# Factor layout, swapped reciprocals and an earlier normalisation in a two-layer graph kernel

## The chip, the cores and the metric

The kernel runs on one core of a Trainium2 chip. A core has five engines that run side by side, each with its own queue of instructions: TensorE for matrix products (PE in the profile, with PEld for loading its weights), VectorE (DVE), ScalarE (ACT), GpSimd (POOL) and SyncE (SP, which here only issues DMAs). ACT issues DMAs as well. The metric is the device time of one execution in microseconds (us), a median over runs.

## What is computed

`x` is 64 graphs of 256 nodes with 512 channels; all graphs share one adjacency matrix. Both layers add a graph layer's output to their input and normalise each row:

```python
# layer 0: a sum over the neighbours, as two products of x
Wi, Wj = (W[:, :Din], W[:, Din:])
mi = jnp.einsum('bkd,od->bko', x, Wi)
mj = jnp.einsum('bkd,od->bko', x, Wj)
out = deg[None, :, None] * (mi + b) + jnp.einsum('ij,bjo->bio', a, mj)
...
# layer 1: attention of 8 heads of 64 channels, masked by the graph
scores = jnp.einsum('bhqd,bhkd->bhqk', q, k) * scale
scores = jnp.where(mask, -jnp.inf, scores)
attn = jax.nn.softmax(scores, axis=-1)
out = jnp.einsum('bhqk,bhkd->bhqd', attn, v)
return out @ Wo.T + bo
...
x = _layernorm(x + layer0(x)); x = _layernorm(x + layer1(x))
```

q, k and v are products of the normalised first layer (called h) with 512 x 512 weights, plus biases. All is in 32 bit floats.

## The kernel before

Two graphs ("batches", index i) are a group g; there are 32 groups. A batch has two tiles of 128 nodes (t = 1 is made before t = 0). The main loop (L1109) runs over the groups. Each turn does the attention of group g (scores, exponentials, values and the division by the softmax sums, eight steps w of two heads each) and, between these, layer 0 of the two batches b1 and b2 of the next group. At its end stand the output projection of group g (`o_steps`), then the v, q and k projections of the next group. Nearly every instruction is recorded with `in_order`, which keeps each engine's instructions in the order of the program text; so that text is each engine's queue, and a wait holds up all that stands behind it on its engine.

**Products in three passes.** The four projections of layer 1 run in fp32r, a faster format of fewer bits than f32. So both sides are split into a head, a low and a diff part. The three products head x head, low x lift and diff x diff go to two PSUM banks: X takes the first and the second, Y the third, and the result is UP times X, plus Y. On the side of the weights the parts (head, lift, diff) are called a factor: 128 rows of 3 x 512 numbers, 16 of them for wv, wq, wk and wo. They are made once, stored to DRAM by `end_makes` into `kept`, and read again in each turn by `bring`, which issues one load of 768 KB on ACT's queue. The ring `stream` has six buffers; `bring` waits until the matmuls have let go of the oldest. For v all four factors are in use at once, and for the output projection too. The parts of the activations are `hP` (tiles hA, hL, hD) for h, and `aoP` for the attention's output `aoT`, whose parts live in buffers that others have left: its head is called qT in the profile, its diff kT, its low part v.

**Banks.** `pair(kind)` takes an X and a Y bank: "S" takes one double bank of the two that the scores use too, "M" takes two of the three single banks, "A" one single bank and the bank of the values. In the profile a matmul into an "S" pair shows as pxy, into the others as px and py. A pair is free again when its two adds have been done (`add_x`, `add_y` in `o_steps`, `v_evict` for v).

**The output projection.** `o_steps` gives three steps: `o[0]` and `o[1]` make tiles 0 and 1 of the group's first batch, 12 matmuls each, with kinds "S" and "M"; `o[2]` makes both tiles of the second batch, 24 matmuls, kinds "A" and "S". Its adds go to DVE, and into `xh`, the residual. `v_pair` follows, kinds "SM" for the first batch (t = 1 takes "M" and comes first) and "AS" for the second (t = 1 takes "S" and comes first).

**How h comes to hP.** A tile is normalised in two parts: `stat` (DVE statistics, then rstd on POOL, L482) and `give` (a shift and a scaling on ACT, L487 and L488). `send_h` (L687) writes it to DRAM, `fetch_h` (L692) reads it back as hB in another order, `turn_h` transposes it on DVE (L506) into hF, and `split_head`, `split_diff`, `split_low` (L665, L668, L671) make its parts. In `o[2]`, between the matmuls, `turn` is called for tile 1 of b2, and its transpose stands on DVE ahead of the adds of the second batch.

**The division.** `values` leaves 128 rows per two steps w: four blocks of 32 channels, for which `channels(q)` gives the order. `divide_two` copies them to `aoT` on ACT; `divide` has PE sum the exponentials of the four heads (tile den, rows of 32 partitions for each), takes the reciprocal on DVE (L974, tile rden) and spreads it by four DMAs (L979) so that each of the four blocks and both of the two steps has its head's reciprocal (tile spread). `multiply` (L925, POOL) then multiplies. Two divisions are made for each batch. For the last of a turn ACT issues half of the DMAs.

The order at the end of a turn, with the lines that the prediction goes through:

```python
        values(g, 7)
        aoP[g][1], = three(("v",))
        split_low(*ao_parts(g, 0, every), nc.gpsimd)
        stat2(1)
        total_up = divide_two(g, 7)
        stat2(0)
        split_low(*ao_parts(g, 1, upper), nc.gpsimd)
        give2(1)
        give2(0)
```

`every`, `upper` and `lower` are all four channel chunks c, the first two, and the last two.

Of the kernel before, what the change touches and what calls it, by code (L numbers as in the profile page):

```python
# [16 lines left out]
P = 128  # L17
# [207 lines left out]
def unshifted_path(ctx, tc, flag, x, adj, wiT, wjT, b0, wqT, bq, wkT, bk, wvT, bv, woT, bo, out):  # L225
# [56 lines left out]
    def in_order(ins):  # L282

        tc.keep_in_program_order(ins)
# [90 lines left out]
    def channels(q):  # L375

        half, j = divmod(q, 2)
        return slice(j * DH + half * R, j * DH + (half + 1) * R)

    def load_wo(t, c0):  # L380
        w = woT.rearrange("(c p) o -> p c o", p=P)
        for q in range(P // R):
            in_order(nc.sync.dma_start(out=t[q * R:(q + 1) * R], in_=w[channels(q), c0:c0 + t.shape[1], :]))

    def small_loads():
        with nc.allow_non_contiguous_dma(reason="512 numbers, once"):
            for q in range(P // R):
                in_order(nc.sync.dma_start(out=bv_t[q * R:(q + 1) * R],
                                           in_=bv.rearrange("r (c p) -> p (r c)", p=P)[channels(q)]))
        in_order(nc.sync.dma_start(out=bo_bc, in_=bo.to_broadcast([P, D])))  # L390
        return load_bias(bq, "bq"), load_bias(bk, "bk")

# [1 line left out]
    bo_bc = const.tile([P, D], F32, name="bo_bc")  # L394

    weights = {"wq": wqT, "wk": wkT, "wv": wvT, "wo": woT}
    kept = {name: dram.tile([NC, P, 3, D], F32, tag=name, name=name) for name in weights}

    raws = {}

# [30 lines left out]
    def bring(several=1, left=1):  # L431
        for _ in range(several):
            if queue:
                name, j, first = queue.pop(0)
                f = stream.tile([P, 3, D], F32R, tag="factor", name="factor")
                coming.append(f)
                if first:
                    begin_make(f, name, j)
                    end_makes(left)
                else:  # L440
                    end_makes()
                    in_order(nc.scalar.dma_start(out=f.bitcast(F32), in_=kept[name][j]))

    def cut(f):
        return [f[:, i, :].rearrange("p (c o) -> p c o", c=NC) for i in range(3)]
# [10 lines left out]
    def end_makes(left=0):  # L456
        while len(started) > left:
            f, low, name, j = started.pop(0)
            head, lift, diff = cut(f)
            in_order(nc.scalar.activation(lift, low, AF.Identity, scale=LIFT))  # L460
            in_order(nc.vector.scalar_tensor_tensor(diff, low, LIFT, head.bitcast(F32), ALU.mult, ALU.subtract))
            in_order(nc.sync.dma_start(out=kept[name][j], in_=f.bitcast(F32)))

    def fold_value_bias():

# [337 lines left out]
                    v_evict(g, i, t, banks[t])  # L803
        return run

    def o_steps(g, kinds, turn):
        parts = aoP[g]

        def add_x(i, t, banks):
            r = xh[NB * g + i][:, t, :]  # L810
            in_order(nc.vector.scalar_tensor_tensor(r, banks[0], UP, r, ALU.mult, ALU.add))

        def add_y(i, t, banks):
            r = xh[NB * g + i][:, t, :]
            in_order(nc.vector.tensor_add(r, banks[1], r))

        def one(t):
            def run():
                banks = pair(kinds[t])
                for which in ((0, 1), (2,)):  # L820
                    for c in range(NC):
                        rows_of_product(banks, parts, t, coming[c], c, which)
                add_x(0, t, banks)
                add_y(0, t, banks)
            return run

        def two():
            banks = [pair(kinds[NT + t]) for t in range(NT)]
            for c in range(NC):
                for which in ((0, 1), (2,)):  # L830
                    for t in range(NT):
                        rows_of_product(banks[t], parts, NT + t, coming[0], c, which)
                coming.pop(0)
                if c:
                    bring()
                if c == 1:
                    bring()
                    h1 = turn(1)
                    split_head(*h1)
                    split_low(*h1, nc.gpsimd)  # L840
            add_x(1, 0, banks[0])
            split_diff(*h1)
            add_y(1, 0, banks[0])
            add_x(1, 1, banks[1])
            add_y(1, 1, banks[1])
            split_three(*turn(0), nc.gpsimd)

        return [one(0), one(1), two]

    def finish_steps(g):  # L850

# [56 lines left out]
    def values(g, w):  # L908
        i, pr = divmod(w, NC)
        if w == 0:  # L910
            aoT[g] = p1.tile([P, NC, NB * N], F32, tag="aoT", name="aoT")
        pp = w % 2
        if pp == 0:
            pavs[g] = value_bank("pav").rearrange("p (r q) -> p r q", r=2)
        pe, _ = made[g, w]
        for kc in range(NT):
            for q in range(P // R):
                d0 = 2 * pr * DH + channels(q).start
                matmul(pavs[g][q * R:(q + 1) * R, pp, :], vv[g][:, i, kc, d0:d0 + R], pe[:, q % 2, kc, :],
                       start=(kc == 0), stop=(kc == NT - 1), tile_position=(0, q * R))  # L920

    def multiply():
# [4 lines left out]
    def divide_two(g, w):  # L927

        dst = target(g, w)
        last = w == NB * NC - 1 and g < NG - 1  # L930
        in_order(nc.scalar.copy(dst, pavs[g]))
        i, pr = divmod(w, NC)
        return divide(dst, [made.pop((g, w - 1))[1], made.pop((g, w))[1]],
                      rtot[:, NB * g + i, pr // 2:pr // 2 + 1], last)

    def total(rden, total_out):
        unused = p1.tile([P, N], F32, tag="unused", name="unused")
# [2 lines left out]
    def divide_at_once(g, w):  # L940


        den = score_bank("den").rearrange("p (r q) -> p r q", r=2)
        for pp in range(2):
            _, pk = made.pop((g, w - 1 + pp))
            for q in range(P // R):
                matmul(den[q * R:(q + 1) * R, pp, :], ones[:, :R], pk[:, q % 2, :], start=True, stop=True,
                       tile_position=(0, q * R))
        inverses = p1.tile([P, 2, N], F32, tag="spread", name="rden")
        for pp in range(2):  # L950
            in_order(nc.vector.reciprocal(inverses[:, pp, :], den[:, pp, :]))
            in_order(nc.vector.tensor_mul(target(g, w)[:, pp, :], pavs[g][:, pp, :], inverses[:, pp, :]))
        return inverses
# [7 lines left out]
        cols = slice(i * N, (i + 1) * N)  # L961
        return cut_parts(aoP[g], cs, cols), aoT[g][:, cs, cols]

    def divide(dst, pks, total_out, last):


        den = bank("den")[:, :N]
        for pp in range(2):
            for j in range(2):
                q = 2 * pp + j  # L970
                matmul(den[q * R:(q + 1) * R, :], ones[:, :R], pks[pp][:, j, :], start=True, stop=True,
                       tile_position=(0, q * R))
        rden = p1.tile([P, N], F32, tag="rden", name="rden")
        in_order(nc.vector.reciprocal(rden, den))  # L974
        spread = p1.tile([P, 2, N], F32, tag="spread", name="spread")
        for half in range(2):
            for pp in range(2):
                issuer = nc.scalar if last and pp else nc.sync
                in_order(issuer.dma_start(out=spread[half * DH:(half + 1) * DH, pp, :],  # L979
                                          in_=rden[pp * DH:(pp + 1) * DH, :]))  # L980
        products.append((dst, spread))
        if last:
            return lambda: total(rden, total_out)
        total(rden, total_out)
# [18 lines left out]

    def projection_steps(g, kinds="", paired=True):
        if paired:
            v = [v_pair(g, 0, "MS"[::-1], False), v_pair(g, 1, "AS", True)]
        else:
            v = [v_step(g, i, t, kinds[NT * i + t], (i, t) == (NB - 1, 0)) for i in range(NB) for t in range(NT)]
        q, k = ([qk_step(g, store, tag, bias, m, kinds[m]) for m in range(NC)]
# [99 lines left out]
    for g in range(NG - 1):  # L1109
# [71 lines left out]
        values(g, 6)  # L1181
        values(g, 7)
        aoP[g][1], = three(("v",))
        split_low(*ao_parts(g, 0, every), nc.gpsimd)
        stat2(1)
        total_up = divide_two(g, 7)
        stat2(0)
        split_low(*ao_parts(g, 1, upper), nc.gpsimd)
        give2(1)
        give2(0)  # L1190
        total_up()
        send_h(b2, 1)
        send_h(b2, 0)
        fetch_h(b2, 1)
        fetch_h(b2, 0)
        split_diff(*ao_parts(g, 1, upper))
        if g + 2 < NG:
            next_p[0][2]()
        h10 = turn_h(b1, 0)
        multiply()  # L1200
        split_head(*ao_parts(g, 1, lower))
        split_head(*h10)
        p, q = next_p, next_q
        v, q_, k = projection_steps(g + 1)
        end = finish_steps(g)
        o = o_steps(g, "SMAS", lambda t: turn_h(b2, t))
        o[0]()
        split_diff(*ao_parts(g, 1, lower))
        split_low(*ao_parts(g, 1, lower), nc.vector)
        split_diff(*h10)  # L1210
        split_low(*h10, nc.vector)
        o[1]()
        run([o[2], v[0]])
        sum_x(b3)
        v[1]()
        turn_x(b3 + 1)
# [107 lines left out]
```

## Time and profile before

| what | value |
|---|---|
| time, median of 3 runs | 2985.07 us (2984.91 to 2987.25) |
| the profiled execution, its own time | 2979.46 us |
| its span, from the first to the last instruction | 2977.2 us |
| granted TensorE clock, mean | 0.998 |
| PE busy / PEld busy | 2934.5 us (99%) / 1917.7 us (64%) |
| DVE / ACT / POOL busy | 2310.1 (78%) / 1194.6 (40%) / 1273.0 us (43%) |
| queue q10 (ACT's DMAs) | 75,808 packets, 391.02 MB, 34.5% of 16 engines |
| queue q1 (SP's DMAs) | 229,584 packets, 215.69 MB, 25.1% |
| hB<-h_cols, issue to landing | 2.5 us least, 3.1 median, 8.0 most |
| one SP issue of spread<-rden | 0.59 us median, 446 of them (62 more on ACT) |

A row of a timeline is: start in us, duration in us, engine, line, operation, output<-inputs by the program's names, shapes, and in brackets how long the engine had been idle and who released it. A row of the waits is: engine, the tile that its instruction writes, its line, the releaser, then us in total, times, longest. "PE MATMUL pxy<-factor,qT" is a matmul of the output projection (with kT: diff; with v: low), "pxy<-factor,hA" (hD, hL) one of the v projection, "pxy<-hA,factor" one of q or k. The line L290 is the helper that records every matmul, so matmuls are told apart by their tiles. A matmul's record is longer than the distance to the next one's start, since they are pipelined; distances between starts say what PE spends.

### The profile page before, as it was taken

The page shows a single profiled execution, that of the slowest core. Times are in us where ns is not written, and L with a number is a line of the kernel's source. Part 1 is how long each engine was busy: PE and PEld are TensorE (multiplying, and loading weights), DVE is VectorE, ACT ScalarE, POOL GpSimd, SP SyncE. Part 2 cuts the span into 40 slices and gives each one's busy share as a digit, 9 for nine tenths or more (in the row PEclk, how much of TensorE's full clock was granted, in tenths as well). Part 3 has the DMA queues.
Part 4 walks back from the last instruction along what each step waited for, and adds up shares of the span by engine and source line. Part 5 has one row for each costly group of instructions (what it writes and reads, how often), then busy time and mean ns, then how long its engine had stood idle before and what let it go on. Part 6 is the DMA issues. An engine that isn't in the chain of part 4 may idle for free. (4 is left out here: it accounts for less than half of the span.)

```text
span 2977.2 us, 42690 instructions
## 1 busy us (share of the span) xinstructions
PE 2934.5 (99%) x15694; PEld 1917.7 (64%) x15694; DVE 2310.1 (78%) x3497; ACT 1194.6 (40%) x2243; POOL 1273.0 (43%) x950
## 2 busy tenths in 40 slices
PE   9999999999999999999999999999999999999998
PEld 5566666666666666666666666666666666666655
DVE  5977787777887778877778777788777787777875
ACT  3433434434434334343343343443433434334333
POOL 3534444344444344443444444444434444344443
PEclk9999999999999999999999999999999999999999
DMA  6566655667555665556665566755566555666553
GB/s 230 172 231 237 217 162 185 222 234 240 178 179 197 235 239 202 167 188 229 236 237 164 177 211 231 245 184 170 197 237 238 201 160 191 232 237 236 166 167 125
DMA packets 305604, 609.48 MB, mean 205 GB/s; under 512 B 27632, under 2 KB 189424, under 8 KB 305136
## 3 DMA queue, kind: packets, MB, share of 16 engines
q10 hardware_dynamic: 75808, 391.02, 34.5%
q1 hardware_dynamic: 229584, 215.69, 25.1%
q8 instruction: 126, 2.06, 0.3%
q14 instruction: 86, 0.70, 0.1%
HBM read 494.67 MB, written 78.64 MB: 193 GB/s over the span
## 5 line engine op out<-in xcount | busy, mean ns | idle before, releaser
L897 POOL TENSOR_TENSOR pk<-pe 128x512 f32<-128x512 f32 x256 | 330.7, 1303 | 534.6 <-ACT pe L887 534.6
L290 PE MATMUL po<-w,xS 128*128 128x512 f32 x992 | 466.1, 602 | 1.5 <-DVE mj L570 1.5
L290 PE MATMUL po<-w,xT 128*128 128x512 f32 x808 | 387.4, 604 | 0.8 <-ACT u L549 0.8
L482 POOL TENSOR_TENSOR rstd<-ve,mhalf 128x1 f32<-128x1 f32 x256 | 155.3, 607 | 493.1 <-DVE below L480 491.9
L887 ACT ACTIVATE pe<-pe 128x1024 f32<-128x1024 f32 x256 | 270.6, 1057 | 148.2 <-DVE pe L883 148.2
L671 POOL TENSOR_TENSOR hL<-hF,hA 128x512 fp32r<-128x512 f32 x93 | 151.2, 1626 | 387.5 <-ACT hA L665 387.5
L290 PEld LDWEIGHTS po<-w,xS 128*128 128x128 f32 x992 | 177.8, 189 | 214.6 <-issue 162.2
L883 DVE TENSOR_TENSOR pe<-ps,maskT 128x1024 f32<-128x1024 f32 x256 | 300.9, 1196 | 3.6 <-PE ps L290 3.6
L759 DVE TENSOR_TENSOR kT<-py,kT 128x512 f32<-128x512 f32 x128 | 88.5, 691 | 259.7 <-ACT kT L758 259.7
L290 PEld LDWEIGHTS po<-w,xT 128*128 128x128 f32 x808 | 145.6, 189 | 180.5 <-issue 179.0
L367 POOL TENSOR_TENSOR xh<-xh,degb 128x1024 f32<-128x1024 f32 x64 | 152.4, 2382 | 254.9 <-DMA xh<-in_x_dram 134.8
L290 PE MATMUL ps<-qT,kT 64*128 64x256 f32 x2048 | 256.5, 389 | 0.0
L290 PE MATMUL pav<-pe,v_sb 128*32 128x256 f32 x4096 | 248.7, 382 | 3.5 <-DVE kT L759 1.5
L290 PEld LDWEIGHTS ps<-qT,kT 64*128 64x128 f32 x2048 | 187.0, 186 | 69.0 <-PE pav L290 38.7
L487 ACT ACTIVATE shift<-below,rstd 128x1 f32<-128x1 f32 x256 | 74.5, 291 | 386.3 <-POOL rstd L482 231.2
L974 DVE RECIPROCAL rden<-den 128x256 f32<-128x256 f32 x127 | 221.9, 1747 | 6.3 <-PE den L290 3.8
L290 PEld LDWEIGHTS pav<-pe,v_sb 128*32 128x32 f32 x4096 | 118.3, 109 | 155.4 <-issue 49.2
L488 ACT ACTIVATE xh<-xh,shift,rstd 128x512 f32<-128x512 f32 x256 | 208.9, 816 | 8.5
L925 POOL TENSOR_TENSOR aoT<-aoT,spread 128x512 f32<-128x512 f32 x127 | 205.7, 1620 | 6.9 <-DMA spread<-rden 5.9
L665 ACT ACTIVATE hA<-hF 128x512 fp32r<-128x512 f32 x124 | 77.8, 628 | 287.1 <-DVE hF L506 231.5
L290 PE MATMUL px<-hA,factor 128*128 128x512 f32 x640 | 184.3, 410 | 0.0
L290 PE MATMUL py<-hD,factor 128*128 128x512 f32 x640 | 176.3, 397 | 2.2 <-ACT kT L758 2.2
(142 smaller groups left out, 6060.1 us busy)
## 6 DMA issues: line engine op xcount, KB each, us to landing
factor<-wv ACTq DMA_DIRECT2D x124, 768.0 KB, 6.3
factor<-wq ACTq DMA_DIRECT2D x124, 768.0 KB, 6.6
factor<-wk ACTq DMA_DIRECT2D x124, 768.0 KB, 6.4
factor<-wo ACTq DMA_DIRECT2D x120, 768.0 KB, 7.2
xB<-in_x_dram SPq DMA_DIRECT2D x256, 128.0 KB, 3.7
xh<-in_x_dram SPq DMA_DIRECT2D x64, 512.0 KB, 8.9
h_cols<-xh SPq DMA_DIRECT2D x124, 256.0 KB, 2.3
hB<-h_cols SPq DMA_DIRECT2D x124, 256.0 KB, 3.1
```

Of the source, the lines that this page charges most:

```text
L290: in_order(nc.tensor.matmul(*args, **kw))
L367: in_order(nc.gpsimd.tensor_tensor(xh[b], xh[b], degb, ALU.add))
L482: order(nc.gpsimd.tensor_tensor(rstd, ve, mhalf, ALU.pow))
L488: order(nc.scalar.activation(t, t, AF.Identity, bias=shift, scale=rstd))
L665: in_order(nc.scalar.activation(parts[0], src, AF.Identity, scale=DOWN))
L671: in_order(engine.tensor_tensor(parts[1], src, parts[0].bitcast(F32), ALU.subtract))
L759: in_order(nc.vector.tensor_add(dst, Y, dst))
L883: in_order(nc.vector.tensor_add(pe.rearrange("p j t q -> p j (t q)"), ps.rearrange("p j t q -> p j (t q)"), maskT.rearrange("p t q -> p (t ...
L887: in_order(nc.scalar.activation(flat, flat, AF.Exp, scale=QSCALE, accum_out=etot[:, NB * g + i, pr:pr + 1]))
L897: in_order(nc.gpsimd.tensor_tensor(pk, pe[:, :, 0, :], pe[:, :, 1, :], ALU.add))
L925: in_order(nc.gpsimd.tensor_tensor(d, d, spread, ALU.mult))
L974: in_order(nc.vector.reciprocal(rden, den))
```

## The change

- The factors in DRAM change from `[NC, P, 3, D]` to `[NC, 3, P, D]`: the three parts of a partition's row no longer lie beside each other, so that each piece in DRAM is 512 numbers, 2 KB, instead of 6 KB. The tile in SBUF is as before.
- The reciprocals are swapped rather than spread: `values` puts the two lower blocks (q = 2, 3) of the two steps in each other's place (`pp ^ (q // 2)`), so that the sums' reciprocals already fit one of the two slots where they stand. They are written to `spread[:, 0]`, and two DMAs, one for each half of the partitions, fill slot 1 with the other half's. The tile rden is gone. The same swap of channels goes into the loading of wo and of the value bias (`chunk_sets`), and into `divide_at_once`. One division near the end uses the buffer "lo".
- At the end of a turn `give2(1)` moves ahead of `divide_two(g, 7)`, and `send_h(b2, 1)` right behind it; `fetch_h(b2, 0)` moves behind the turning of h10 and the multiply.
- The low part of `aoP` for the first batch is made in two pieces, `upper` and `lower`, with `give2(1)` between them.
- `o_steps` gives `own`, `adds` and `others`. `own` makes both tiles of the first batch into "S" pairs, the low products of tile 0 put between and behind the first products of tile 1; `adds(0)` now stands ahead of `turn_h(b1, 0)` on DVE. `others` takes "A" and "M". The v pairs are "SS" and "AM" (with "AM", t = 1 takes "M" and comes first).

```diff
+    def chunk_sets(q):
+        return ((0, 1), (1, 0)) if q > 1 else ((0, 0),)
...
-    kept = {name: dram.tile([NC, P, 3, D], F32, tag=name, name=name) for name in weights}
+    kept = {name: dram.tile([NC, 3, P, D], F32, tag=name, name=name) for name in weights}
...
-                    in_order(nc.scalar.dma_start(out=f.bitcast(F32), in_=kept[name][j]))
+                    in_order(nc.scalar.dma_start(out=f.bitcast(F32), in_=kept[name][j].rearrange("k p d -> p k d")))
...
-            in_order(nc.sync.dma_start(out=kept[name][j], in_=f.bitcast(F32)))
+            in_order(nc.sync.dma_start(out=kept[name][j].rearrange("k p d -> p k d"), in_=f.bitcast(F32)))
...
+        def own():
+            for n, cs in ((0, (0, 1)), (1, (2, 3))):
+                banks[n] = pair("S")
+                times(n, range(NC), (0, 1))
+                times(0, cs, (2,))
+            times(1, range(NC), (2,))
+
+        def adds(n):
+            add_x(n)
+            add_y(n)
+
+        def others():
+            banks.update({2: pair("A"), 3: pair("M")})
...
-                matmul(pavs[g][q * R:(q + 1) * R, pp, :], vv[g][:, i, kc, d0:d0 + R], pe[:, q % 2, kc, :],
+                matmul(pavs[g][q * R:(q + 1) * R, pp ^ (q // 2), :], vv[g][:, i, kc, d0:d0 + R], pe[:, q % 2, kc, :],
...
-        rden = p1.tile([P, N], F32, tag="rden", name="rden")
+        spread = p1.tile([P, 2, N], F32, tag="lo" if other else "spread", name="spread")
+        rden = spread[:, 0, :]
         in_order(nc.vector.reciprocal(rden, den))
-        spread = p1.tile([P, 2, N], F32, tag="spread", name="spread")
         for half in range(2):
-            for pp in range(2):
-                issuer = nc.scalar if last and pp else nc.sync
-                in_order(issuer.dma_start(out=spread[half * DH:(half + 1) * DH, pp, :],
-                                          in_=rden[pp * DH:(pp + 1) * DH, :]))
+            issuer = nc.scalar if last and half else nc.sync
+            in_order(issuer.dma_start(out=spread[half * DH:(half + 1) * DH, 1, :],
+                                      in_=spread[(1 - half) * DH:(2 - half) * DH, 0, :]))
...
-            v = [v_pair(g, 0, "MS"[::-1], False), v_pair(g, 1, "AS", True)]
+            v = [v_pair(g, 0, "SS", False), v_pair(g, 1, "AM", True)]
...
-        split_low(*ao_parts(g, 0, every), nc.gpsimd)
+        split_low(*ao_parts(g, 0, upper), nc.gpsimd)
         stat2(1)
+        give2(1)
+        split_low(*ao_parts(g, 0, lower), nc.gpsimd)
         total_up = divide_two(g, 7)
+        send_h(b2, 1)
         stat2(0)
         split_low(*ao_parts(g, 1, upper), nc.gpsimd)
-        give2(1)
         give2(0)
         total_up()
-        send_h(b2, 1)
         send_h(b2, 0)
         fetch_h(b2, 1)
-        fetch_h(b2, 0)
         split_diff(*ao_parts(g, 1, upper))
         if g + 2 < NG:
             next_p[0][2]()
+        own, adds, others = o_steps(g, lambda t: turn_h(b2, t))
+        own()
+        adds(0)
         h10 = turn_h(b1, 0)
         multiply()
         split_head(*ao_parts(g, 1, lower))
         split_head(*h10)
+        fetch_h(b2, 0)
...
-        o[0]()
         split_diff(*ao_parts(g, 1, lower))
         split_low(*ao_parts(g, 1, lower), nc.vector)
         split_diff(*h10)
         split_low(*h10, nc.vector)
-        o[1]()
-        run([o[2], v[0]])
+        adds(1)
+        others()
+        v[0]()
```

## The prediction

> **What bounds the kernel now.** Parts 1 and 2 of the page come first: PE is busy 99% of the span, and the granted clock is 9 tenths or more in every slice. Part 4 (the chain that ended last) names only the last layer norm, so it doesn't help. The Trainium skill ("Perfetto Trace Analysis", Identifying the Most-Contended Engine) says that matmul busy time is a poor measure of how near PE is to its peak, since matmuls are pipelined. The trace agrees in a way that matters here: weight loading (PEld) is at 64%, and matmuls of 0.39 us start every 0.227 us. Busy time would leave under 43 us to gain (2977.2 - 2934.5). So I read starts in the timeline instead. Each turn of the main loop has the same 142 stretches of matmuls; at their undisturbed intervals (0.227 us for 512 columns of fp32r, 0.429 for a record of f32, and the usual 1.93, 1.75 and 0.55 us for a group of scores, values and sums) they need 88.07 us. The 29 periods measured from the trace take 90.7 us at least and 91.6 on average, in all 102 us over the ideal. About 77 us of it repeats every period (2.6 each), 25 us does not.
>
> Where is it? In PE's waits, these three kinds lead:
>
> ```profile
> PE pxy L290 <- DVE xh L815: 7.9, 4, 3.1
> PE pxy L290 <- POOL v L671: 6.5, 31, 0.9
> PE px L290 <- DMA factor<-wv: 4.1, 8, 1.0
> ```
>
> All three lie in the output projection and the v projection behind it. I call the first matmul of `o_steps` the boundary, and count us from it; the one at 1238.53 is undisturbed. PE's timeline there:
>
> ```profile
> 1240.55 0.39 PE L290 MATMUL pxy<-factor,kT 128*128 128x512 f32 x1
> 1241.12 1.20 PE L290 MATMUL pxy<-factor,v 128*128 128x512 f32 x4 [0.18 <-POOL v L671]
> ...
> 1247.83 0.39 PE L290 MATMUL py<-factor,kT 128*128 128x512 f32 x1
> ...
> 1250.32 0.39 PE L290 MATMUL px<-factor,hA 128*128 128x512 f32 x1
> 1250.73 0.50 PE L290 MATMUL py<-factor,hD 128*128 128x512 f32 x1
> ```
>
> The step from 1240.55 to 1241.12 is 0.57 us instead of 0.23, and the four from there take 1.03 (the next starts at 1242.15) instead of 0.91: **0.46 us lost, every period (0.48 on average)**. The listed idle time is only 0.18, because a matmul's record runs on for 0.16 after the next could start, and 0.1 goes in restarting. The steps from 1250.32 to 1250.73 and on to 1251.06 are 0.41 and 0.33, and lose 0.18 + 0.11: **0.30 a period**. The step at 1247.83 loses nothing, but it is the one to watch.
>
> **Part 1: the low half of `aoP` in two pieces.** The first loss waits for this POOL work:
>
> ```profile
> 1238.66 2.40 POOL L671 TENSOR_TENSOR v<-aoT,qT 128x1024 fp32r<-128x1024 f32 x1
> ...
> 1242.63 0.99 POOL L482 TENSOR_TENSOR rstd<-ve,mhalf 128x1 f32<-128x1 f32 x1 [1.06 <-DVE below L480]
> 1243.59 1.31 POOL L671 TENSOR_TENSOR v<-aoT,qT 128x512 fp32r<-128x512 f32 x1
> 1244.85 1.30 POOL L925 TENSOR_TENSOR aoT<-aoT,spread 128x512 f32<-128x512 f32 x1
> ```
>
> The tile `v` is the low part, ready at 2.53 (1241.06). Halved, the upper piece (1.31, as at 1243.59) is ready at 1.44; PE asks after 8 matmuls, at 2.25. Then comes rstd of h tile 1 (0.55) and the lower piece, ready at 3.3; `own` asks for it after 18 matmuls, at 4.5. So 0.48 goes.
>
> **What is late next.** PE then arrives 0.48 earlier at the matmul of 1247.83, the first to read the lower `diff` (kT) of batch 1. That comes from a chain the change leaves alone: rstd, low piece, multiply (the POOL rows above), ACT head until 1246.82, DVE:
>
> ```profile
> 1246.85 0.69 DVE L668 SCALAR_TENSOR_TENSOR kT<-qT,aoT 128x512 fp32r<-128x512 f32 x1 [0.67 <-ACT qT L665]
> ...
> 1249.98 0.69 DVE L815 TENSOR_TENSOR xh<-py,xh 128x512 f32<-128x512 f32 x1
> ```
>
> kT ends at 1247.54. Where it came late in the trace (the boundary at 508.2) PE followed it by 0.06 and lost 0.11 in restarting. So PE can pass at 1247.60 and not at 1247.35: 0.25 + 0.11 = 0.36 is given back. Part 1 alone is worth 0.12.
>
> **Part 2: other banks.** The loss at 1250.32 is v's first pair ("M") waiting until `add_y` of h tile 1 has emptied it (the DVE row ends at 1250.67, py starts at 1250.73). With "SS" the first pair is the one that `adds(0)` emptied long before; the second is asked for 3 matmuls later, at 12.3 in the new order, when `adds(1)` ended at 12.15. **0.30 goes.** `adds(0)` can't start before 20 of own's matmuls (5.1), DVE is free at 5.3: nothing is lost. "AM" for batch 1 needs `add_x` of tiles 2 and 3, done at 15.1 in this boundary, two us before use.
>
> Parts 1 and 2: (0.48 - 0.36 + 0.30) x 31 = **13.0 us**; the last boundary (at 2884.64), whose first loss is 1.1 rather than 0.34, adds about 0.9.
>
> **Part 3: `give2(1)` and its send earlier.** The boundary at 320.64 shows what it is worth:
>
> ```profile
> 332.10 0.69 DVE L815 TENSOR_TENSOR xh<-py,xh 128x512 f32<-128x512 f32 x1
> 337.23 1.14 DVE L506 STREAM_TRANSPOSE hF<-hB 128x512 f32<-128x512 f32 x1 [4.44 <-DMA hB<-h_cols]
> 338.34 0.39 PE L290 MATMUL pxy<-factor,hL 128*128 128x512 f32 x1
> 341.82 0.77 PE L290 MATMUL pxy<-factor,hA 128*128 128x512 f32 x1 [3.10 <-DVE xh L815]
> ```
>
> DVE stands still for hB, its adds are late, PE waits 3.3 us and then loses 1.5 more in matmuls at 0.43 us. Such losses come at four of the 30 boundaries: 4.8, 0.4, 2.1 and 4.4 = 11.7 us. SP's timeline has the send at 5.45, the fetches at 9.95; in the good boundary at 5.47 and 7.83. New: `give2(1)` needs rstd (2.0 on POOL), then 0.29 + 0.82 on ACT: 3.2; SP issues one spread DMA (0.59) at 3.1 and the send at 3.75, **1.7 us earlier**. The fetch stands behind the other tile's send (6.5, unchanged), so it goes at 6.9 if h_cols has landed: 0.9 earlier than in a good boundary, up to 3 in a bad one, and before the two factor loads at 7.9 and 9.3. I take **11 us**. Behind `give2(1)` on ACT wait the copy of pav (now until 3.7; its bank is wanted at 5.8) and ACT's spread DMA (3.7 rather than 3.1).
>
> **Part 4: swapped reciprocals.** Two DMAs instead of four (508 to 254), each 0.59 us of issue. At three of four divisions nobody on PE's path waits. At the last, the two queues end issuing at 4.3 instead of 4.5, so the multiply keeps its POOL slot at 6.3. At five boundaries it started 0.35 to 1.1 late, and PE lost 2.5 in all; I take **1.5** of that. The reciprocal now waits for the multiply before it (one buffer): at the second division 1216.6 against 1217.79, at the others more, so nothing. The swapped channels need six more DMAs in the setup (bv 4 to 6, wo 8 to 12), 0.57 us of SP each, 3.4 in all, between 28.8 and 43.7 us; behind them stand stores of factors that are first read after 100 us, and none of PE's waits before 140 us names a DMA: nothing either.
>
> **Part 5: factors in rows of 2 KB.** The packet records give a median of 234 ns for 6144 bytes and 84 for 2048: 252 against 234, over 62,976 packets and 16 engines +71 us of DMA time, hidden under engines that are 5 to 7 tenths busy. The path it could reach is the wv load at 9.27, read at 16.18: 6.9 us, against
>
> ```profile
> factor<-wv ACTq DMA_DIRECT2D x124, 768.0 KB, 6.3
> ...
> xh<-in_x_dram SPq DMA_DIRECT2D x64, 512.0 KB, 8.9
> ```
>
> Where it was late, PE lost 6.8 us in ten boundaries. A rule speaks against the change: "DMA: Bandwidth & Descriptors", Why small descriptors are slow, has about 3 cycles and 32 bytes per descriptor; in beats of 32 bytes that is 204 for 196, +4% by my estimate, where the records say +8%. By either, two loads in flight take 3.7 us of engine time plus 0.2 or 0.3. Against that: hB's packets (2 KB) no longer stand behind 6 KB ones. The same page (Queues, rings and completion order) has each engine alternate between queues by packet. hB's 8 packets per engine would then take 8 x (84 + 234) = 2.5 us now and 1.35 after; the trace has 2.5 from issue to landing at best and 8.0 at worst, so 5.5 of waiting: the sharing is poorer than the rule's. Bounds: all 6.8 gone; or 62 us lost, if a factor landed like xh (8.9: 2.0 past the slack, 31 times). The 2 KB packet's own 84 ns is the nearer row, and h leaves earlier: I take **3.4 gained**.
>
> Sum: 13.0 + 0.9 + 11 + 1.5 + 3.4 = **30 us**. The profiled execution took 2979.5 (span 2977.2); it would take 2949.5. The runs' median is 5.6 above it, carried over unchanged: **2955**.
>
> **Rivals.** (a) The DVE and POOL chain decides: DVE is 94% busy from the boundary to 17.5 (16.45 of 17.54 us). If ACT's later spread DMA or the h_cols write beside it delays the multiply by 0.5, kT delays PE as much: 31 x 0.5 = 15, **2970**. For it: the multiply had no gap after POOL's work, so spread's margin is unseen. Against: fewer issues. (b) hB lands as late as before: the 11 and 3.4 stay, **2969**. (c) kT's give-back is smaller and late wv loads vanish: 11 + 3.4 more, **2941**. (d) Slower: the three-row factor load lands too late for the wait after 1254. The margin is 0.6 over the median; from about 7.9 us on, a stall of 1.0 at each of 31 boundaries eats the whole gain, and at xh's 8.9 it costs 62: **3017**. For it: xh's landing. Against: xh lands slowly while its small packets share engines with 6 KB ones, which go. (e) No change: gains and a small (d) cancel.
>
> **How the numbers follow.** Mine 0.50 (2948 to 2963), (a) or (b) 0.27, (c) 0.12, (d) 0.05, (e) 0.06. The range 2938 to 2974 leaves out (d), (e) and tails. A change below 0.2% (6 us) can't be told from none: faster 0.90, same 0.05, slower 0.05.
>
> **What would show it.** Right: the steps at 2.0 and 11.8 are 0.227 and a new one of about 0.4 stands at the first lower kT; DVE's wait for hB is near zero; the best period falls from 90.7 to 90.3 and the mean to about 90.6. Wrong: wv waits at every boundary, or a multiply later than 6.4.

## The result, and the profile after

The changed kernel takes **2960.65 us** (median of 6 runs, 2957.51 to 2965.63) against 2984.97 for the kernel before (6 runs, 2977.5 to 2987.25) in the same series: a ratio of 0.9922, 95% interval 0.9908 to 0.9935, or 24.3 us less. The prediction was 2955, with 2938 to 2974 as its range, and 2948 to 2963 for its likeliest case. The total came out. Its division among the parts did not, and that took the experiments to see.

The profiled execution took 2960.62 us (span 2958.8); before it was 2979.46. Three views answer to those shown of before. First PE's waits, in the same columns (total, times, longest), and the landing times with the queue of ACT's loads:

```profile
PE pxy L290 <- DMA factor<-wv: 12.1, 22, 1.1
```

```profile
q10 hardware_dynamic: 199280, 388.99, 37.6%
...
factor<-wv ACTq DMA_DIRECT2D x124, 768.0 KB, 7.2
...
factor<-wo ACTq DMA_DIRECT2D x120, 768.0 KB, 9.5
...
xh<-in_x_dram SPq DMA_DIRECT2D x64, 512.0 KB, 7.8
```

The waits for the adds (xh L815) and for the low part v are gone from the list. The wait for wv stands alone at its top and has tripled (it was 4.1 us, 8 times). A wv factor lands in 7.2 us instead of 6.3.

PE's timeline at the boundary of 868.08 shows which steps of the prediction came true (start, duration, then output<-inputs; the distance between starts is what counts):

```profile
870.08 0.39 PE L290 MATMUL pxy<-factor,kT 128*128 128x512 f32 x1
870.31 0.62 PE L290 MATMUL pxy<-factor,v 128*128 128x512 f32 x2
870.76 0.39 PE L290 MATMUL pxy<-factor,qT 128*128 128x512 f32 x1
...
876.66 0.39 PE L290 MATMUL px<-factor,qT 128*128 128x512 f32 x1
877.12 0.50 PE L290 MATMUL py<-factor,kT 128*128 128x512 f32 x1
877.46 0.40 PE L290 MATMUL px<-factor,qT 128*128 128x512 f32 x1
...
879.78 0.39 PE L290 MATMUL pxy<-factor,hA 128*128 128x512 f32 x1
880.01 0.39 PE L290 MATMUL pxy<-factor,hD 128*128 128x512 f32 x1
...
884.03 0.40 PE L290 MATMUL pxy<-factor,hL 128*128 128x512 f32 x1
885.42 0.50 PE L290 MATMUL pxy<-factor,hA 128*128 128x512 f32 x1 [1.00 <-DMA factor<-wv]
```

The step into the first low product (870.08 to 870.31) is 0.23, and two of them take 0.45: nothing is lost. The v projection starts (879.78 to 880.01) at 0.23: nothing lost. At the first lower kT the steps are 0.46 and 0.34, 0.23 + 0.11 over, where 0.36 was predicted. Then the fourth wv factor comes late: 1.39 instead of 0.23.

SP's queue at the same boundary, and the instructions on hB:

```profile
871.18 0.51 SPq L991 DMA_DIRECT2D spread<-spread  x1
871.74 2.98 SPq L696 DMA_DIRECT2D h_cols<-xh  x2
874.81 2.37 SPq L701 DMA_DIRECT2D hB<-h_cols  x2
```

```profile
  DMA hB<-h_cols: 0.3, 1
...
DMA to landing us min/median/max: 2.5/2.9/7.0
```

The send goes at 3.66 after the boundary and the fetch at 6.73 (6.9 predicted). DVE's wait for hB fell from 19.6 us to 0.3.

To compare kernels I measured, in every trace, how much each of the 96 matmuls from the boundary starts over 0.227 us behind the one before, as a mean over the 30 boundaries. In us per period ("own" contains a step of 0.41 at its start that all kernels have):

| kernel | best / mean period | own | others | v, batch 1 | v, batch 2 |
|---|---|---|---|---|---|
| before | 90.65 / 91.55 | 0.92 | 0.09 | 0.87 | 0.17 |
| before, second profile | 90.66 / 92.00 | 0.92 | 0.05 | 1.14 | 0.37 |
| parts 1 and 2 alone | 90.92 / 91.51 | 0.44 | 0.41 | 0.33 | 0.89 |
| part 4 alone | 90.69 / 90.93 | 0.93 | 0.00 | 0.47 | 0.00 |
| parts 1 to 4 (rows of 6 KB) | 90.28 / 90.76 | 0.44 | 0.35 | 0.44 | 0.01 |
| changed kernel | 90.33 / 91.02 | 0.43 | 0.37 | 0.68 | 0.01 |

What these kernels lose outside these 96 matmuls is about 1.4 to 1.5 a period in all of them. The best period, 90.33, is the predicted 90.3. The mean is 91.0 and not 90.6: that difference is the late wv (most of the 0.68).

### The profile page after: what moved, and what is told of

It reads as the page before. It is cut to its first block, busy times and chain, and to the rows that moved or that the text cites. A ratio compares the mean times of both kernels' runs of the same rounds, so it can differ in the third digit from the quotient of the medians.

```text
span 2958.8 us, 42319 instructions
## 1 busy us (share of the span) xinstructions
PE 2921.7 (99%) x15694; PEld 1914.3 (65%) x15694; DVE 2296.8 (78%) x3497; ACT 1197.1 (40%) x2243; POOL 1275.0 (43%) x981
## 5 line engine op out<-in xcount | busy, mean ns | idle before, releaser
L988 DVE RECIPROCAL spread<-den 128x256 f32<-128x256 f32 x127 | 222.0, 1748 | 3.8 <-PE den L290 3.0
```

## The experiments

All ratios are to the kernel before in the same series. That kernel itself scattered from 2978 to 2992 in 38 runs; medians of the three series were 2985.33, 2985.73 and 2984.35. The parts are numbered as in the prediction: 1 low half in two pieces, 2 other banks, 3 earlier normalisation and send, 4 swapped reciprocals, 5 rows of 2 KB.

| kernel | median us (range) | ratio [95%] |
|---|---|---|
| parts 1, 2 | 2978.96 (2974.2 to 2981.03) | 0.9975 [0.9965, 0.9986] |
| parts 1, 2, 4 | 2956.04 (2955.2 to 2958.9) | 0.9898 [0.9883, 0.9913] |
| parts 1, 2, 3, 4 | 2951.33 (2949.4 to 2953.6) | 0.9885 [0.987, 0.99] |
| parts 1, 2, 4, 5 | 2955.78 (2952.97 to 2957.09) | 0.9901 [0.9886, 0.9916] |
| all, again | 2957.2 (2956.66 to 2959.43) | 0.9902 [0.9887, 0.9918] |
| part 5 alone | 2975.2 (2971.17 to 2976.97) | 0.9965 [0.9951, 0.9978] |
| part 4 alone | 2957.68 (2957.3 to 2959.44) | 0.9913 [0.9897, 0.9928] |
| before, again | 2986.12 (2978.25 to 2989.89) | 0.9994 [0.9986, 1.0003] |
| all, low piece earlier | 2967.86 (2966.99 to 2972.46) | 0.9943 [0.9929, 0.9956] |
| all, other v order | 2942.17 (2941.39 to 2942.94) | 0.986 [0.9842, 0.9878] |
| parts 1 to 4, other v order | 2941.41 (2940.82 to 2943.3) | 0.9856 [0.9838, 0.9874] |
| the same, low piece earlier | **2937.15** (2936.42 to 2940.27) | 0.9845 [0.9829, 0.9861] |

### The layout: does it cost or help?

The changed kernel with the old rows of 6 KB, and the kernel before with the new rows of 2 KB:

```diff
-    kept = {name: dram.tile([NC, 3, P, D], F32, tag=name, name=name) for name in weights}
+    kept = {name: dram.tile([NC, P, 3, D], F32, tag=name, name=name) for name in weights}
...
-                    in_order(nc.scalar.dma_start(out=f.bitcast(F32), in_=kept[name][j].rearrange("k p d -> p k d")))
+                    in_order(nc.scalar.dma_start(out=f.bitcast(F32), in_=kept[name][j]))
...
```

> The changed kernel with the factors' layout undone (rows of 6 KB). Theory: the longer landing of wv (7.2 us instead of 6.3) comes from the 2 KB rows, so it returns to about 6.3, PE's waits for wv fall from 12.1 us in 22 boundaries to under 5, the mean loss behind the third wv factor falls from 0.6 to 0.2 us a period, and the time is 8 to 13 us below the changed kernel (about 2950). DVE's wait for hB stays under 2 us because of the earlier fetch. Rival: wv is late because h's traffic now shares the engines at that moment; then the waits stay near 12 us, and with 6 KB rows ahead of hB the waits of DVE for hB come back (over 5 us), and the time is equal to the changed kernel or up to 8 us above.

> The kernel before with the layout alone (rows of 2 KB). Theory: wv lands at about 7.2 us and is late in most boundaries, PE's waits for wv rise from 4.1 us to 12 or more; hB's worst landing falls from 8.0 us, so DVE's wait for hB falls from 19.6 us to under 10, which gives some of it back: net 0 to 8 us slower than before. Rival (the layout is what helped hB): DVE's wait for hB falls under 3 us, wv stays as it was, and the time is 8 to 12 us less than before.

Taken out of the changed kernel, the rows of 2 KB give 6 to 9 us back (2951.33 against 2960.65 and 2957.2; the 10 runs of the one, 2956.66 to 2965.63, and the 4 of the other don't overlap). PE's wait for wv, 12.1 us with the rows of 2 KB, is now

```profile
PE pxy L290 <- DMA factor<-wv: 5.9, 11, 1.2
```

Put into the kernel before, the same rows *gain* 10 us: the rival's time, but not its reason. There the factors were late as well: PE waits 8.0 us for wv instead of 4.1. DVE's wait for hB hardly fell (17.7 us, against 19.6 and 27.9 in the two profiles of before; both expectations had it under 10), but PE's wait for xh fell to 5.2 us from 7.9 and 12.5. So the rows of 2 KB do two opposite things, and which one shows depends on what else is late.

### The order: what is the earlier send worth?

`give2(1)` and `send_h(b2, 1)` back in their old places, all else as changed; once with rows of 2 KB, once with 6 KB:

```diff
-        give2(1)
...
-        send_h(b2, 1)
...
+        give2(1)
         give2(0)
         total_up()
+        send_h(b2, 1)
```

> The changed kernel with the second normalisation of tile 1 and its send back at their old place. Theory (the earlier send is what took hB off the path): the first hB fetch goes back from 6.74 to about 7.8 us after the boundary, DVE's wait for hB comes back at some boundaries (5 to 15 us in all), and the time is 5 to 12 us above the changed kernel. Rival (2 KB rows alone keep hB on time): DVE's wait for hB stays under 2 us and the time is the same within 3 us.

> Parts 1, 2 and 4 alone: the changed kernel with rows of 6 KB and with the normalisation and send of tile 1 at their old place. If both undone parts cost time on their own, the time is 5 us or more below the changed kernel with 6 KB rows alone (2951), that is 2940 to 2947, with PE's waits for wv under 4 us. If the late send only looked cheaper because 2 KB rows let hB through beside the factors, hB is late again with 6 KB rows: DVE waits for it 10 us or more, and the time is 2951 to 2960.

With rows of 6 KB the earlier send is worth 4.7 us (2956.04 to 2951.33), as the second alternative of that run had it; with rows of 2 KB nothing, perhaps a small loss (2955.78 without it, 2957.2 and 2960.65 with it): the waits for hB come back as expected, the time does not. DVE's wait for hB is 11.6 us (6 KB) and 7.3 us (2 KB) without it and 0.3 us in the changed kernel, so it does what it was meant for, but little is left to do. And it has a cost. Without it, and with the rows of 2 KB still in place, PE's 12.1 us for wv fall to

```profile
PE pxy L290 <- DMA factor<-wv: 3.7, 10, 0.7
```

This settles what the rows cost: with the late send nothing (2955.78 against 2956.04), with the early one 6 to 9 us. The fourth wv factor lands at 15.6 us after the boundary with neither, 15.8 with the rows of 2 KB, 16.0 with the earlier send, 16.3 with both (medians), and PE needs it at about 15.7. So the late wv of the changed kernel is the work of parts 3 and 5 together, and the rival of the run with 6 KB rows, h's traffic beside the loads, was half right. How the earlier send delays that load is not shown.

### Parts 1 and 2 alone

The kernel before with `own`, `adds`, `others`, the pairs "SS" and "AM", and the low half in two pieces; the sends, reciprocals and rows as before.

> The kernel before with parts 1 and 2 alone (low part in two pieces, own and others, the new banks), without the earlier normalisation, the swap and the layout. Theory: the two repeated losses go and 0.33 us comes back at kT: the shortest period is 90.3, and the waits of DVE for hB and of PE for wv stay as in the kernel before: 9 to 15 us less than before. Rival: PE, 0.4 us earlier, only runs into hB and wv more often, and under 5 us remain.

6.8 us came of the 13.9 in the sum, between the theory and the rival. The own products lost 0.44 instead of 0.92 and the bank loss went, as predicted. But h now came late at every boundary. The fetch at the boundary of 1237.02, DVE's wait for hB, and what it leads to on PE, a wait for the low part of h that its list of before does not have:

```profile
1244.84 1.38 SPq L692 DMA_DIRECT2D hB<-h_cols  x2
```

```profile
DVE hF L506 <- DMA hB<-h_cols: 36.1, 31, 3.5
...
PE px L290 <- POOL hL L671: 14.3, 27, 0.6
```

The fetch goes at 7.82 after the boundary, unchanged; its median over all boundaries is 7.84. But ACT issues the first wv load at a median of 7.81 (7.91 before): the new order of the products frees that buffer 0.1 us earlier. So the load of 768 KB now goes 0.03 us *ahead* of the fetch, where it went 0.07 behind, and this fetch lands in 5.3 us (median) instead of 4.0. The second wv load is issued earlier too, at 8.79 instead of 9.27, but the order alone can account for it: at the four boundaries of the two profiles of before where the first load happened to go 0.11 to 0.13 ahead, the fetch took 5.1 to 5.5 us, with the second load as late as 1.06 to 1.09 behind it.

### Part 4 alone

The kernel before with the swapped reciprocals (and the swap of channels that goes with them), and nothing else:

```diff
-            for pp in range(2):
-                issuer = nc.scalar if last and pp else nc.sync
-                in_order(issuer.dma_start(out=spread[half * DH:(half + 1) * DH, pp, :],
-                                          in_=rden[pp * DH:(pp + 1) * DH, :]))
+            issuer = nc.scalar if last and half else nc.sync
+            in_order(issuer.dma_start(out=spread[half * DH:(half + 1) * DH, 1, :],
+                                      in_=spread[(1 - half) * DH:(2 - half) * DH, 0, :]))
...
```

> The kernel before with the swapped reciprocals alone (two DMAs a division instead of four; rows of 6 KB, the old order). Theory: the last division's multiply keeps its slot and a few late ones go, 0 to 5 us less: 2980 to 2985. Rival: SP is freed of 0.59 us of issue at the boundary, so that the send and the fetch of h go earlier and the waits for hB shrink: 10 us less, about 2975, with DVE's wait for hB under 10 us.

Both theories were far too low: it gained **26.7 us**, as much as the whole change (24.3, and 28.5 in the second series). The rival had what happened on SP, at a third of the size. SP's queue at the worst boundary of the kernel before (320.64), and then at the same turn (319.26) with the swap:

```profile
323.77 1.38 SPq L979 DMA_DIRECT2D spread<-rden  x2
326.09 1.40 SPq L687 DMA_DIRECT2D h_cols<-xh  x2
330.59 1.06 SPq L692 DMA_DIRECT2D hB<-h_cols  x2
```

```profile
322.36 0.51 SPq L987 DMA_DIRECT2D spread<-spread  x1
324.06 1.83 SPq L696 DMA_DIRECT2D h_cols<-xh  x2
326.43 2.79 SPq L701 DMA_DIRECT2D hB<-h_cols  x2
```

SP issues the second spread DMA no more, so the send goes at 4.80 after the boundary instead of 5.45, and the fetch at 7.17 instead of 9.95. Over all boundaries the median fetch is at 7.17, now 0.74 ahead of the first wv load, and the latest at 7.46 (9.96 before). In DVE's rows on hB:

```profile
  DMA hB<-h_cols: 3.0, 5
...
DMA to landing us min/median/max: 2.5/2.7/7.8
```

3.0 us of waiting against 19.6 and 27.9 in the two profiles of before, and 36.1 with parts 1 and 2. The waits for the adds are gone from PE's list, and in the table above the v projection falls from 1.04 and 1.51 to 0.47. That the swap alone suffices is shown; whether the 0.63 us by which SP sends earlier or the halved traffic of the reciprocals in the us before it does more, no run separates.

Added to parts 1 and 2 instead, the same edit takes 22.9 us off (2978.96 to 2956.04).

### The give-back at kT

POOL's low piece of batch 1 ahead of the statistics of tile 0, in the changed kernel:

```diff
-        stat2(0)
         split_low(*ao_parts(g, 1, upper), nc.gpsimd)
+        stat2(0)
```

> The changed kernel with one row moved: the low piece of batch 1 goes ahead of the statistics of tile 0 on POOL, so it runs in POOL's gap. Theory (kT gives back 0.33 us a period because the chain rstd, low piece, multiply is late): the multiply starts about 0.3 us earlier or when spread lands, the 0.33 us at the first lower kT shrinks to between 0 and 0.1, the best period falls from 90.33 to about 90.05, and the time is 7 to 10 us below the changed kernel. Rival (spread's landing sets the multiply, not POOL): the multiply starts at the same moment, the 0.33 us stays, and the time is the same or, since rstd of tile 0 comes 0.5 us later and with it the send of tile 0, up to 4 us above.

POOL's timeline at the boundary of 1233.69 and PE's waits:

```profile
1236.85 1.30 POOL L680 TENSOR_TENSOR v<-aoT,qT 128x512 fp32r<-128x512 f32 x1
...
1239.22 1.29 POOL L938 TENSOR_TENSOR aoT<-aoT,spread 128x512 f32<-128x512 f32 x1
```

```profile
PE pxy L290 <- DMA factor<-wv: 27.8, 38, 1.9
```

The multiply starts 5.53 after the boundary instead of 6.3, and the loss at the lower kT is gone: 0.02 a period in others instead of 0.37. So that chain was indeed the second limit, as the prediction had it. Yet the kernel is 7 to 11 us slower: PE loses 1.40 a period in the v projection of batch 1 instead of 0.68. PE comes 0.33 earlier to wv, and the loads end later: the first is issued at 8.13 instead of 7.78, and the second lands 16.7 after the boundary instead of 16.3 (medians).

### A later need of wv

If the wait for wv is what is left, PE should need the factors later. `v_pair` makes both tiles of batch 1 chunk by chunk, all four chunks; now six matmuls of batch 2's tile 1 stand ahead of the fourth:

```diff
+            for c in range(NC - 1):
+                for t in (1, 0):
+                    rows_of_product(first[t], hP[g], t, coming[c], c)
+            ahead = pair("M")
+            for c in (0, 1):
+                rows_of_product(ahead, hP[g], NT + 1, coming[c], c)
+            for t in (1, 0):
+                rows_of_product(first[t], hP[g], t, coming[NC - 1], NC - 1)
...
```

> The changed kernel with the old rows of 6 KB, and the v projection in another order: the first two channel chunks of both tiles of batch 1, and the third, then the first two chunks of batch 2's tile 1, and only then the fourth, so that 6 matmuls (6 x 0.227 = 1.36 us) more lie between PE's coming and its first need of the late wv factors. Theory (what was left at the boundary is the wait for wv): with 6 KB rows in the old order PE lost 0.39 us a period there (0.31 waiting and 0.08 restarting), 30 x 0.39 = 12; most of it goes, so about 2941 (2938 to 2945), and PE's wait for wv falls from 5.9 us to under 1. Rival: the pair of banks that batch 2's tile 1 takes is emptied by the adds only 15.7 us after the boundary, so it becomes the wait in place of wv: no gain, 2949 to 2954, with PE's wait now for DVE xh at the line of the adds.

> The changed kernel with its rows of 2 KB and the v order. Theory (all that the rows of 2 KB cost goes through the wait for wv): with that wait gone, the time is within 2 us of the same kernel with rows of 6 KB, about 2941 (2938 to 2946), 14 to 20 below the changed kernel. Rival: rows of 2 KB cost elsewhere too (other loads, the setup), and it stays 6 us or more above the one with 6 KB rows: 2947 or more.

> The same, and the lower low piece of batch 1 moved ahead of the statistics of tile 0, as in the earlier experiment that took the loss at the first lower kT (0.33 us a period) away and gave it back at wv. Theory: with the later need of wv it is no longer given back: 0.33 x 31 = 10 us below the run with the v order alone, about 2931 (2928 to 2936). Rival: wv or the banks bind again at once, and it is given back as before: 2938 to 2944, equal to the v order alone.

The first two did as their theories said: with rows of 6 KB the new order is worth 9.9 us (2951.33 to 2941.41), with 2 KB 15 to 18 (2957.2 and 2960.65 to 2942.17). PE waits no more for wv, nor for the adds, in either; the longest wait left is a single one at 74.61, before the main loop:

```profile
PE py L290 <- ACT kT L767: 1.9, 1, 1.9
```

That is the kernel with rows of 6 KB; the one with 2 KB has the same line at its top. Though its wv factors land in 7.0 us instead of 6.4, they differ by 0.8 us with ranges that overlap. So all that the rows of 2 KB cost went through this one wait.

The third gained 4.3 of the 10 expected. The loss at kT is gone (0.02 a period in others), but 0.15 comes back in the v projection, part of it at the banks:

```profile
PE py L290 <- DVE xh L851: 3.0, 3, 1.1
```

It is the fastest kernel of the study, 2937.15 us, 47 below the kernel before and 20 to 24 below the changed one.

### The same kernels again

> The kernel before once more, for a second profile of it. The profiled execution of before (2979.5 us) was 5.5 us under the median of its runs. Theory: the waits that come and go (DVE for hB, PE for wv) are larger in an ordinary execution: about 6 us more in these two, the repeated losses (0.46 and 0.30 us a period) unchanged, shortest period 90.65. Rival: the repeated part differs, the shortest period is longer by 0.2 us.

> The changed kernel once more, on the same chip as the others of this call. Theory: 2957 to 2963 us, PE waits 8 to 15 us for wv. Rival (the first profile was an unlucky one): under 2955, with waits for wv under 6 us; then neither the 6 KB rows nor the late send gained anything.

The profile of before fell on a slower execution this time (2989.89 us against 2979.46). The repeated part is the same, as expected (own 0.92, best period 90.66). The extra time is mostly late h: DVE waits 27.9 us for hB instead of 19.6, PE 12.5 for xh instead of 7.9 (and 7.3 for wv instead of 4.1). A second part of the cost shows only in the granted clock. Behind the wait of 3.10 us for xh at 341.82 the first profile has (window, length, busy time of PE, PEld, DVE, ACT and POOL, then the granted clock, here 0.50):

```profile
341.40:344.80 3.40, 2.98 (x7) 2.43 (x8) 2.70 (x5) 1.60 (x3) 1.34 (x1) 0.50 0.70 291
```

The matmuls there start 0.43 us apart instead of 0.227; the prediction saw them and counted their cost, but not that it comes with the clock. In the two profiles all six waits for xh of 2.57 us or more were followed by such a stretch, of 3.4 or 6.8 us; in the main loop they make 6.8 us in the first profile and 20.5 in the second. A PE that is busy loses half of that, some 3 and 10 us by my estimate, so about 7 of the 10.4 us between the two executions. The changed kernel and the one with part 4 alone have no such stretch in the main loop. The mean granted clock tells the same of executions without a profile: 0.995 to 0.999, mostly 0.997, in the 38 of the kernel before, and 0.998 or 0.999 in all ten of the changed kernel. A difference of 0.002 over 2977 us is 6 us, so about a quarter of the gain is, by this estimate, clock that late h no longer costs.

The changed kernel's second profile repeats the first (own 0.44, others 0.36, v of batch 1 0.58).

## Why the prediction was right, and where it wasn't

**Parts 1 and 2 (13.9): each step held, the sum did not.** The low products lose nothing, the bank loss is gone, and 0.33 comes back at kT where 0.36 was predicted; the low piece moved ahead confirms that chain. Alone, though, they are worth 6.8: PE's progress frees the buffer for the first wv load 0.1 us earlier, and that load then beats the fetch of h. The prediction had the load's issue in view only as something that the fetch should pass, not as something that its own part 1 moves.

**Part 3 (11) and part 4 (1.5): the causes were exchanged.** "At three of four divisions nobody on PE's path waits. At the last, the two queues end issuing at 4.3 instead of 4.5" looked for who waits for the reciprocals. The instruction that waited was the next one on SP: the send of h. The prediction had this 0.59 us and used it, but inside part 3 ("SP issues one spread DMA (0.59) at 3.1 and the send at 3.75, 1.7 us earlier"), and gave the whole gain to the 1.7. The runs show that part 4 suffices, with the send only 0.63 earlier: it is worth 26.7 alone and 22.9 behind parts 1 and 2, and part 3 adds 4.7 with rows of 6 KB and nothing with 2 KB. The gain at hB itself is as predicted: the waits are gone.

**Part 5 (3.4 gained): the mis-sized term, with the wrong sign in this order.** The rest of the sum used the packets' own time, 252 ns for 234. What counts is the landing with h, x and a second factor in flight: 7.2 us for 6.3 (+14%), and 9.5 for 7.2 for wo, while xh's loads on SP's queue, whose packets were never large, got faster (8.9 to 7.8). The prediction kept landing at its old median and saw 0.6 us of margin. Measured, the median landing of the fourth factor went from 16.06 to 16.33 after the boundary, while PE's need of it came from 16.2 to 15.7 (66 intervals of 0.227 and the losses ahead: 0.41 + 0.46 + 0.30 before, 0.41 + 0.33 after): the gain of parts 1 and 2 is what moved PE towards it. So rival (d) did happen, at a small size, and the prediction's own sign of being wrong, waits for wv at every boundary, came at 22: PE loses 0.60 a period instead of 0.24 for waiting and restarting, or 0.36 x 31, some 11 us. With rows of 6 KB it is 0.38, so the rows are 0.22 x 31, 7 us, of it, in keeping with the 6 to 9 of the runs. But the prediction weighed them alone. They cost this only with part 3's earlier send, which delays the same load; without it they cost nothing. Where the prediction weighed the Trainium skill ("DMA: Bandwidth & Descriptors", Why small descriptors are slow) against the packet records, +4% by the one and +8% by the other, both were right in sign, and neither tells the +14% and +32% of a load among others. The other use of that page (Queues, rings and completion order) took one record of the trace for the page's packet, which is typically of 9 to 17 descriptors. At the boundary of 320.64 the trace shows coarser turns: hB, fetched at 9.95 and 10.7 behind both wv loads, had none of the 256 records of its two fetches start before 13.0.

The second half of part 5's reasoning, that hB's packets no longer stand behind 6 KB ones, fits the kernel before, where the fetch of tile 1 landed in 3.2 us (median) instead of 4.0; but DVE's wait for hB fell little, and how much of the 10 us gained there is due to it is not shown. With h sent earlier there was nothing for it to do.

**The sum: two errors that cancel.** That the total fell into the likeliest case is in part luck. Against its own profiled execution the kernel got 18.8 us faster, not 30. But "the runs' median is 5.6 above it, carried over unchanged" failed too, in the other direction: the changed kernel's profile (2960.62) is its median (2960.65). What stood between the profile and the median of before was late h and the half clock behind it, which the change removes. 11.1 too slow in the profile and 5.6 less carried over leave the 5.65 (rounded) by which the forecast missed.

One detail: the text says the factors are first read after 100 us; the trace has the first load at 87. No wait came of it.

## What to carry to other kernels

An instruction that is removed can be worth more through what stands behind it in its queue than through what waits for its result: ask what the next instruction on that queue is, and against which other transfer it races. Where several edits relieve the same wait, don't add their gains; give the wait to the smallest one that removes it, and price the others at what is left. And when an edit brings an engine earlier to its next need, set that need beside the end of the transfer it reads, since a load that does not end earlier turns the gain into a wait; two edits that are each harmless to that load can be late together.

## What was not expected of the hardware

- A race of 0.1 us decides. With the fetch of h's tile 1 issued 0.03 us behind a load of 768 KB on the other queue (parts 1 and 2), it landed in 5.3 us (median); 0.07 ahead of it (before) in 4.0; 0.74 ahead (part 4 alone) in 2.8. Behind both wv loads (0.2 to 0.7 us behind the second, four boundaries in the two profiles of before) it took 6.6 to 8.0.
- Issuing a load earlier need not make it land earlier: the fourth wv factor is issued at 9.27 in the kernel before and at 8.79 with rows of 6 KB and parts 1 to 4, and lands at 16.06 and 15.97; with the late send, also issued at 8.79, at 15.6.
- Smaller rows on one queue shift time to the other: with rows of 2 KB for the factors, loads of 512 KB on SP's queue took 7.8 to 8.0 us in all kernels here, with 6 KB 8.8 to 9.0; the factors' loads went the other way (wo 9.3 to 9.9 us with 2 KB, 7.2 to 7.5 with 6 KB).
- A wait of PE of 2.57 us or more for xh was followed, six times out of six in the two profiles of before, by 3.4 or 6.8 us at a granted clock of 0.5; the one of 1.93 us was not.
